# Three edits to a four-layer graph kernel: ScalarE issues the tile loads, the planner books the DMA engines, layer 3's product is split in three passes, and GpSimd alone adds the last h

## The chip, the cores and the metric

The kernel runs on one core of one Trainium2 chip. The metric is the device time of one execution in microseconds; the time of a kernel is the median of its runs. A profiled execution has a time of its own, a little beside that median.

## The reference

128 graphs of 128 nodes, 256 features each, float32, and a 0/1 adjacency matrix `adj` for each graph. Four layers follow each other, and each adds to x what it makes of h = relu(layernorm(x)):

- layer 0 is a gated graph network of three steps. In each step m = h W[i], the messages are summed over neighbours (`A^T m`), and a GRU cell with 768 gate columns makes the next h from the sums and from h. The last h is added to x.
- layer 1 is a relational sum: for every relation r of 4, a mask `adj == r` sums h over neighbours, and the sum goes through its own weight. With a 0/1 `adj` only r = 1 has any edges. A bias is added.
- layers 2 and 3 are graph attention: Wh = h W, scores e = leaky_relu(a1 Wh_i + a2 Wh_j), masked by `adj`, softmax over neighbours, and the weighted sum of Wh. They differ only in what a masked score becomes.

```python
x = x + _L0_gnn_ref(h, adj, weight, w_ih, w_hh, b_ih, b_hh)   # three GRU steps
x = x + _L1_gnn_ref(h, L1_adj, adj, L1_weight, L1_bias)       # masks (adj == r), r = 1..4
x = x + _L2_gnn_ref(h, adj, L2_W, L2_a)                       # attention, masked by -inf
x = x + _L3_gnn_ref(h, adj, L3_W, L3_a)                       # attention, masked by -9e15
```

## The kernel before

**Tiles.** Four graphs make a group (G = 4), so there are 32 groups, and a tile holds 128 partitions by 512 columns (T). In layer 0 the GRU's products are done with h turned, features on the partitions: `wide` tiles hold h so. In layers 1 to 3 a "duo" of two graphs shares one product (`product`, two graphs by 256 columns).

**Split products.** A float32 product on TensorE is emulated, where it matters, by three passes in the fp32r format: a matrix is split into a high part, a low part and their difference (`forms`: lines 944 to 966, `product`: lines 785 to 838). The high part is rounded by ScalarE or VectorE (L955, L957, L806, L808), the low part is made by VectorE (L961, L811) and the difference by GpSimd or VectorE (`difference`, L470). Passes 0 and 1 run, the result in PSUM is multiplied by 1 + 2^-12 (`rescale` L1011 and L1013 in layer 0, `scale` L828 and L830 in `product`, with a bias L1005), and pass 2 is added on top. All GRU gates are done so (L992, 216 passes of 512 columns a group). `THIN = (1, 2)` says that the products with the weights of layers 1 and 2 are done so too (L819, passes of 256 columns); layer 3's is a plain fp32 product (L775), whose left side is copied out of PSUM first (`evict`, L461). The last two groups (PLAIN) use plain products everywhere.

**Other steps that are named later.** L974 sums over neighbours in layer 0, L765 in layers 1 to 3. `norm` makes statistics on VectorE (L696 and the small steps L710 to L726), a power on GpSimd (L722) and the scaled relu on ScalarE (L743). The gates' tanh is on ScalarE (L1023, L1040), the GRU's update on VectorE (L1035, L1042, L1045, L1048). Attention scores are made on VectorE (L1119, L1170, L1173) and ScalarE (L1166, L1179), and VectorE adds the attention's result to x (L1210).

**Turns.** `turn` transposes 32x32 blocks on VectorE (L490), writes the tile to DRAM (`give`, L493) and reads it back with the blocks exchanged (`take`, L502, four DMAs). That is how h changes from features on partitions to nodes on partitions after each step, and how the attention matrix is turned. After the last step the turned h is added to x by VectorE or GpSimd, whichever the planner picks (`residual`, L1080).

**DMA queues.** Only SyncE issues DMAs, but for four weight loads at the start, which ScalarE issues. On SyncE's queue stand, in the planner's order: the loads of x (L513, twice for each group: once for layer 0 and, into another buffer, once again for the sum), of `adj` (L531, and again for the masks L524), of `adjT` (L1095), the turns, the row of attention terms that goes through DRAM (L1151, L1153), and the stores of the result (L1220). DMAs use eight completion semaphores in turn, so each waits until the one eight before it has landed. A load also waits until its buffer is free; there are three x buffers and five `adj` buffers, and an x buffer is often freed by the store of an earlier group.

**The order of the work.** No engine's order is written by hand. `build` records every operation with its engine (or a choice of engines), an estimate in ns and what it reads and writes. `Plan.order` then simulates the engines: it takes, again and again, the ready operation that could start first, and between operations of one engine that could start within `NEAR` ns the one with the lowest rank. The rank is made of the longest chain to the group's end, of the group's number times `PERIOD`, and of a table `OFFSETS` with a number for each place in the code, which was tuned. `LAG`, `HOP`, `OWN` and `late` say how long after an operation another engine, or the same one, sees its result; for a DMA, `LAG` says 4500 ns for SyncE and each call adds its own `late`. GpSimd's operations, and VectorE's operations with `port=True`, are planned so that they do not overlap (`port`). Up to `AHEAD` groups are in flight. The order that comes out is the order in which each engine's instructions are issued, and buffers are given out in it.

**Start and end.** While the weights are split, the whole of `adj` is scanned (L668, L670) for values over 1; a branch (L1236) then takes the program for 0/1 matrices, which is the one that runs, or a general one. The last group is worked in single graphs, the one before it in pairs, to shorten the end.

## Time and profile before

| | |
|---|---|
| median of 3 runs | 2342.71 us (2341.92 to 2347.65) |
| profiled execution | 2353.06 us, span 2351.2 us |
| TensorE matmul busy | 2291.9 us (97%), 12137 records |
| VectorE, ScalarE, GpSimd busy | 1978.2, 1582.0, 912.4 us |
| HBM | 114 GB/s over the span, DMA engines busy about half the time |

How to read it: an fp32 matmul leaves two records in the trace, a split pass one. Matmuls are pipelined, so their durations overlap and their sum is more than the time they take; the time from one start to the next is the pitch. "PEld" is the load of the stationary side, which overlaps the matmuls. Issues of DMAs are not counted as busy. A row of waits names who waited, at which line, for whom.

### The profile page before, as it was taken

The numbers are of one execution on the slowest core, as the hardware profiler recorded it, in microseconds if no ns is written. First come the engines' busy times: TensorE is split into PE (matmuls) and PEld (weight loads), VectorE is DVE, ScalarE is ACT, GpSimd is POOL, SyncE is SP. The second block draws the span as 40 slices with busy tenths as digits, with TensorE's granted clock in tenths as the row PEclk, the third lists the DMA queues.
The fourth block names the chain that finished last, engine by engine and source line by source line (L and its number), as shares of the span: only waits on it lengthen the run. The fifth ranks groups of instructions, "written<-read, shape, count | busy, mean of one in ns | idle before, by whom it ended". The sixth has DMA issues, their size and how long they took to land.

```text
span 2351.2 us, 39064 instructions
## 1 busy us (share of the span) xinstructions
PE 2291.9 (97%) x12137; PEld 1947.2 (83%) x12137; DVE 1978.2 (84%) x5405; ACT 1582.0 (67%) x3272; POOL 912.4 (39%) x729
## 2 busy tenths in 40 slices
PE   7999999999999999999999999999999999999997
PEld 6788888888888888888888888888888888788885
DVE  7858888888888888888888888888888888888887
ACT  6566676766676666666666766666766666666665
POOL 2334334443334443334343334343334343344421
PEclk9999999999999999999999999999999999999999
DMA  8535445555445455455455455455554555545431
GB/s 249 143 83 110 96 90 124 117 128 116 102 110 125 111 133 113 100 117 117 114 126 118 107 115 115 114 129 116 108 115 112 118 122 109 128 103 118 105 77 43
DMA packets 951273, 270.36 MB, mean 115 GB/s; under 512 B 677008, under 2 KB 939280, under 8 KB 951056
## 3 DMA queue, kind: packets, MB, share of 16 engines
q1 hardware_dynamic: 949968, 266.72, 50.0%
q8 instruction: 99, 1.62, 0.3%
q14 instruction: 118, 0.97, 0.2%
q10 hardware_dynamic: 1088, 1.05, 0.1%
HBM read 168.96 MB, written 98.69 MB: 114 GB/s over the span
## 4 chain that ended last, share of the span: by engine, by line
PE 64%; DVE 14%; DMA 10%; ACT 6%; SPq 4%; issue 3%; DVEq 0%; POOL 0%; ACTq 0%
PE bank L992 40%; PE bank L819 7%; PE bank L765 6%; PE bank L974 5%; PE bank L775 5%; DMA swap<-big 4%; SPq L502 4%; DMA big<-swap 3%; DVE junk L1119 3%; DVE form L961 2%; DMA wide<-swap 2%; ACT big L743 1%; DVE wide L1042 1%; DVE wide L1045 1%; DVE big L490 1%
## 5 line engine op out<-in xcount | busy, mean ns | idle before, releaser
L992 PE MATMUL bank<-form,wh_s 128*128 128x512 f32 x3456 | 953.4, 396 | 8.7 <-ACT bank L1005 4.6
L992 PE MATMUL bank<-form,wi_s 128*128 128x512 f32 x3456 | 944.0, 393 | 1.6 <-ACT bank L1013 0.9
L470 POOL TENSOR_TENSOR form<-form,form 128x512 fp32r<-128x512 f32 x383 | 517.7, 1362 | 800.4 <-DVE form L961 565.0
L992 PEld LDWEIGHTS bank<-form,wi_s 128*128 128x128 f32 x3456 | 644.1, 188 | 143.6 <-ACT bank L1013 3.1
L992 PEld LDWEIGHTS bank<-form,wh_s 128*128 128x128 f32 x3456 | 631.8, 188 | 151.5 <-ACT bank L1005 15.8
L1013 ACT ACTIVATE bank<-bank 128x512 f32<-128x512 f32 x448 | 255.4, 574 | 325.7 <-PE bank L992 324.4
L722 POOL TENSOR_TENSOR small<-small,nhalf 128x4 f32<-128x4 f32 (+2 forms) x140 | 142.2, 1020 | 408.8 <-DVE small L720 338.9
L1119 DVE CUSTOM_DVE_ANT_0 junk<-big,ub 128x256 bf16<-128x256 f32 x512 | 244.5, 478 | 14.2 <-ACT big L743 0.5
L743 ACT ACTIVATE big<-xs,small 128x256 f32<-128x256 f32 x384 | 200.1, 590 | 21.6 <-DVE small L726 12.2
L696 DVE BATCH_NORM_STATS2 small<-xs 128x6 f32<-128x256 f32 x512 | 190.0, 415 | 7.3 <-DMA xs<-in_x_dram 6.0
L470 POOL TENSOR_TENSOR cform<-cform,cform 128x512 fp32r<-128x512 f32 x120 | 155.2, 1294 | 96.2 <-DVE cform L811 83.0
L490 DVE STREAM_TRANSPOSE big<-wide 128x512 f32<-128x512 f32 x252 | 173.1, 697 | 4.0 <-ACT wide L743 2.3
L1035 DVE SCALAR_TENSOR_TENSOR bank<-big,bank 128x512 f32<-128x512 f32 x192 | 131.9, 690 | 48.5 <-PE bank L992 35.9
L955 ACT ACTIVATE form<-wide 128x512 fp32r<-128x512 f32 x179 | 109.2, 626 | 83.7 <-DMA wide<-swap 43.4
L1179 ACT ACTIVATE big<-big,small 128x128 f32<-128x128 f32 x256 | 99.8, 392 | 70.0 <-DVE small L1173 69.7
L1023 ACT ACTIVATE bank<-bank,b_rz 128x512 f32<-128x512 f32 x192 | 123.4, 655 | 34.0 <-PE bank L992 30.1
L1210 DVE SCALAR_TENSOR_TENSOR xs<-bank,small,xs 128x256 f32<-128x256 f32 x256 | 118.4, 475 | 31.6 <-PE bank L775 23.0
L1042 DVE TENSOR_TENSOR wide<-wide,bank 128x512 f32<-128x512 f32 x192 | 126.9, 682 | 21.4 <-ACT bank L1040 21.1
L765 PE MATMUL bank<-big,big 128*128 128x128 f32 x1024 | 130.7, 277 | 11.9 <-DVE wide L1045 7.1
L1023 ACT ACTIVATE big<-bank,b_rz 128x512 f32<-128x512 f32 x192 | 130.1, 681 | 16.3 <-PE bank L992 12.1
L765 PEld LDWEIGHTS bank<-big,big 128*128 128x128 f32 x1024 | 123.1, 192 | 19.4 <-DVE wide L1045 9.9
L974 PE MATMUL bank<-adjs,big 128*128 128x128 f32 x1024 | 131.2, 276 | 6.4 <-DMA big<-swap 5.1
(105 smaller groups left out, 3297.5 us busy)
## 6 DMA issues: line engine op xcount, KB each, us to landing
swap<-big SPq DMA_DIRECT2D x312, 256.0 KB, 2.5
big<-swap SPq DMA_DIRECT2D x992, 64.0 KB, 2.3
xs<-in_x_dram SPq DMA_DIRECT2D x128, 256.0 KB, 3.1
adjs<-in_adj_dram SPq DMA_DIRECT2D x64, 256.0 KB, 3.4
wide<-swap SPq DMA_DIRECT2D x128, 128.0 KB, 3.6
big<-line SPq DMA_DIRECT2D x60, 256.0 KB, 3.9
out_dram<-xs SPq DMA_DIRECT2D x30, 512.0 KB, 3.1
big<-in_adj_dram SPq DMA_DIRECT2D x32, 256.0 KB, 4.0
```

Source lines behind the costliest of these rows:

```text
L470: (nc.gpsimd if eng == "POOL" else nc.vector).tensor_tensor(at(df), at(lo).bitcast(F32), at(hi).bitcast(F32), ALU.subtract)
L490: nc.vector.transpose(part.t, src())
L696: op("DVE", dve(D), lambda g=g: nc.vector.bn_stats(s.t[:, ST + 6 * g : ST + 6 * g + 6], xt.t[:, g, :]), r=[(xt, {g})], w=[(s, {("mv", g)})])
L743: nc.scalar.activation(place(g), xt.t[:, g, :].rearrange("p (k m) -> p k m", k=KC), AF.Relu, bias=s.t[:, MR + g : MR + g + 1], scale=s.t[: ...
L765: nc.tensor.matmul(ps.t[:, (len(gs) * k + j) * P : (len(gs) * k + j + 1) * P], hs[g // 2].t[:, (g % 2) * D + k * P : (g % 2) * D + (k + 1) ...
L819: nc.tensor.matmul(po.t[:, j * D : (j + 1) * D], fs[f].t[:, (len(gs) * k + j) * P : (len(gs) * k + j + 1) * P], w.t[:, f, k, :], start=(st ...
L974: nc.tensor.matmul(pg.t[:, g * P : (g + 1) * P], of()[:, g * P : (g + 1) * P], flags(m0)[:, g * P : (g + 1) * P], start=True, stop=True,)
L992: nc.tensor.matmul(ps.t, w.t[(slice(None), *row, j, k, slice(c * P, (c + 1) * P))], b.t, start=(start and x == 0), stop=(x == len(terms) - ...
L1013: nc.scalar.mul(ps.t, ps.t, by)
L1023: op("ACT", act(T, 1), lambda: nc.scalar.activation(to.t, ps.t, AF.Tanh, bias=b_rz.t[:, c : c + 1], scale=0.5), r=[b_rz, *([ps] if kept el ...
L1042: op("DVE", dve(T), lambda c=c, ps=ps: nc.vector.tensor_tensor(hT.t[:, c, :], hT.t[:, c, :], ps.t, ALU.subtract), r=[ps], w=[(hT, {c})])
L1119: nc.vector.tensor_tensor_reduce(out=junk.t, in0=part, in1=ub[i].t[:, v, :], op0=ALU.mult, op1=ALU.add, scale=1.0, scalar=0.0, accum_out=s ...
```

## The change

- `QUEUE = "ACT"`: a new helper `arrive` issues the loads of x, `adj` and `adjT` (now at one line, `arrive`) from ScalarE's queue and not from SyncE's. The scan's loads, the other weights, the turns and the stores stay on SyncE.
- The planner keeps a time `engines` at which the DMA engines are free. An operation recorded for SP or ACTQ gets a size `dma` in ns (`moves`); it takes its place on them behind those placed before, and is seen `LAND` = 1400 ns, its own `late` and the usual hop later. An operation of another engine is seen at its end plus the usual hop; the loads are recorded for "ACT", with a `late` of `LANDING` = 4700 and `moves` = 800. The lags of 4500 and 2500 ns go. An issue is 530 ns and not 470, the estimates of ScalarE's and VectorE's operations rise by 6 or 7 ns, L1119's from 850 to 880, and a GpSimd operation may start `EASE` = 400 ns before VectorE's port is free in the plan.
- `THIN = (1, 2, 3)`: layer 3's product is split in three passes, and its weight with it.
- `residual` is GpSimd's alone.
- `PERIOD`, `CLOSE`, `SOON`, `NEAR` and all 24 rows of `OFFSETS` have new values, so the order of every engine is a new one.

```diff
 PE_COL = 430 / 512
-LAG = {"PE": 165, "ACT": 110, "DVE": 85, "POOL": 20, "SP": 4500, "ACTQ": 2500}
+LAG = {"PE": 165, "ACT": 110, "DVE": 85, "POOL": 20, "SP": 0, "ACTQ": 0}
 HOP = {"PE": 110, "ACT": 40, "DVE": 40, "POOL": 80, "SP": 100, "ACTQ": 100}
...
-OWN = {"PE": 0, "ACT": 125, "DVE": 125, "POOL": 80, "SP": 2500, "ACTQ": 2500}
-PERIOD = 29902
-CLOSE = 7183
+OWN = {"PE": 0, "ACT": 125, "DVE": 125, "POOL": 80, "SP": 0, "ACTQ": 0}
+PERIOD = 36412
+CLOSE = 18983
 CLOSING = 2
-SOON = -210
+SOON = 243
 AHEAD = 5
...
 SPLIT = 2
-LINE, SPREAD = 0, -1000
-GIVE = -400
-TAKE = -2500
+LAND = 1400
+LINE, SPREAD = 1300, 100
+GIVE = 0
+TAKE = 0
 TENSOR = ()
+ISSUE = 530
+EASE = 400
+LANDING = 4700
+ARRIVAL = 2300
+QUEUE = "ACT"
 BLOCK = 32
-NEAR = 69
+NEAR = 42
 RUSH = 90000
...
 DEEP = 1
-THIN = (1, 2)
+THIN = (1, 2, 3)
 LASTS = 4
...
 def seen(o, h):
-    return o.late + (LAG[o.eng] + HOP[h.eng] if h.engs != (o.eng,) else OWN[o.eng])
+    return (o.late + LAND + o.dma if o.dma is not None else 0) + (LAG[o.eng] + HOP[h.eng] if h.engs != (o.eng,) else OWN[o.eng])
...
 def act(n, ptrs=0):
-    return 50 + 95 * ptrs + 0.833 * n
+    return 57 + 95 * ptrs + 0.833 * n
...
 def dve(n):
-    return 68 + n / 0.96
+    return 74 + n / 0.96
...
 def dma(kb):
-    return 470
+    return ISSUE
...
 OFFSETS = {(stage, site): ns for stage, all_ in {
...
 }.items() for site, ns in enumerate(all_)}
...
 class Op:
-    __slots__ = ("engs", "eng", "times", "ns", "fn", "deps", "heirs", "bufs", "group", "key", "port", "rush", "late", "rank", "wait", "ready", "end", "most", "tag")
+    __slots__ = ("engs", "eng", "times", "ns", "fn", "deps", "heirs", "bufs", "group", "key", "port", "rush", "late", "dma", "rank", "wait", "ready", "end", "seen", "most", "tag")
...
-    def op(self, eng, ns, fn, r=(), w=(), after=(), port=None, rush=0, late=0):
+    def op(self, eng, ns, fn, r=(), w=(), after=(), port=None, rush=0, late=0, moves=None):
...
         o.rush, o.late, o.most = rush, late, self.most
+        o.dma = (300 if moves is None else moves) if o.engs[0] in ("SP", "ACTQ") else None
         if self.shared:
...
         at = dict.fromkeys(LAG, 0.0)
-        port = 0.0
+        port = engines = 0.0
...
         def place(o, eng, end):
-            nonlocal first, port
+            nonlocal first, port, engines
             for e in o.engs:
...
             o.end = at[eng] = end
+            o.seen = end
+            if o.dma is not None:
+                n = P // BLOCK if o.ns == ISSUE * P // BLOCK else 1
+                engines = max(max(engines, end - (n - 1) * ISSUE) + o.dma, end + o.dma / n)
+                o.seen = engines + LAND + o.late
             if o.port and eng != "ACT":
-                port = max(port, end)
+                port = max(port, end - (EASE if eng == "POOL" else 0))
             for b in o.bufs:
...
                 if not b.left and id(b.pool) in free:
-                    last = max(u.end + u.late + LAG[u.eng] + 60 for u, _, _ in b.uses)
+                    last = max(u.seen + LAG[u.eng] + 60 for u, _, _ in b.uses)
                     free[id(b.pool)][b.slot] = last
             for h in o.heirs:
-                h.ready = max(h.ready, o.end + seen(o, h))
+                way = LAG[o.eng] + HOP[h.eng] if h.engs != (o.eng,) else OWN[o.eng]
+                h.ready = max(h.ready, o.seen + way)
                 h.wait -= 1
...
                         continue
-                    start = max(at[eng], r, port if o.port and eng != "ACT" else 0)
+                    start = max(at[eng], r, port - (EASE if eng == "POOL" else 0) if o.port and eng != "ACT" else 0)
                     key = (start if start > at[eng] + NEAR else 0, o.rank)
...
                 op("DVE", dve(T) + 15, within, r=[r], w=[part])
-                op("SP", 470, give, r=[part], w=[(swap, {k})], late=GIVE)
+                op("SP", ISSUE, give, r=[part], w=[(swap, {k})], late=GIVE, moves=600)
...
-            op("SP", 470 * P // BLOCK, take, r=[swap], w=[w], late=TAKE)
+            op("SP", ISSUE * P // BLOCK, take, r=[swap], w=[w], late=TAKE, moves=1680 * n - 80 * (n - 1))
             return w
...
         state = {}
+
+        def arrive(dst, src, w, after=()):
+            on_act = QUEUE == "ACT"
+            op(QUEUE, dma(256), lambda: (nc.scalar if on_act else nc.sync).dma_start(out=dst(), in_=src), w=w,
+               after=after, late=LANDING if on_act else ARRIVAL, moves=800)
...
             for g2 in range(G // 2):
-                op("SP", dma(256), lambda g2=g2: nc.sync.dma_start(
-                    out=xt.t[:, 2 * g2 : 2 * g2 + 2, :],
-                    in_=x[ds(gi * G + 2 * g2, 2)].rearrange("g n d -> n g d")),
-                   w=[(xt, {2 * g2, 2 * g2 + 1})], after=after)
+                arrive(lambda g2=g2: xt.t[:, 2 * g2 : 2 * g2 + 2, :],
+                       x[ds(gi * G + 2 * g2, 2)].rearrange("g n d -> n g d"), [(xt, {2 * g2, 2 * g2 + 1})], after)
             return xt
...
             ai = Buf(adjs, f"again{gi}")
-            op("SP", dma(256), lambda: nc.sync.dma_start(
-                out=ai.t.rearrange("p (g j) -> p g j", g=G),
-                in_=adj[ds(gi * G, G)].rearrange("g i j -> i g j")), w=[ai], after=after)
+            arrive(lambda: ai.t.rearrange("p (g j) -> p g j", g=G),
+                   adj[ds(gi * G, G)].rearrange("g i j -> i g j"), [ai], after)
             return ai
...
             xt, ai = fetch(gi, "x0_"), Buf(adjs, f"adj{gi}")
-            op("SP", dma(256), lambda: nc.sync.dma_start(
-                out=ai.t.rearrange("p (g j) -> p g j", g=G),
-                in_=adj[ds(gi * G, G)].rearrange("g i j -> i g j")), w=[ai])
+            arrive(lambda: ai.t.rearrange("p (g j) -> p g j", g=G),
+                   adj[ds(gi * G, G)].rearrange("g i j -> i g j"), [ai])
             state[gi] = xt, ai
...
             if first:
-                op("ACTQ", dma(kb), lambda: nc.scalar.dma_start(out=dst(), in_=src), w=[buf])
+                op("ACTQ", dma(kb), lambda: nc.scalar.dma_start(out=dst(), in_=src), w=[buf], late=ARRIVAL, moves=3.1 * kb)
             else:
-                op("SP", dma(kb), lambda: nc.sync.dma_start(out=dst(), in_=src), w=[buf], rush=rush)
+                op("SP", dma(kb), lambda: nc.sync.dma_start(out=dst(), in_=src), w=[buf], rush=rush, late=ARRIVAL, moves=3.1 * kb)
...
             op("SP", dma(256), lambda part=part, f=f: nc.sync.dma_start(
-                out=part.t.bitcast(I32), in_=flat[:, f * T : (f + 1) * T]), w=[part])
+                out=part.t.bitcast(I32), in_=flat[:, f * T : (f + 1) * T]), w=[part], late=ARRIVAL, moves=800)
             op("DVE", dve(T), lambda part=part, f=f: nc.vector.tensor_reduce(
...
                 for k, h in enumerate(hs_new if i == L - 1 else ()):
-                    def residual(eng, k=k, h=h):
+                    def residual(k=k, h=h):
                         part = xt.t[:, :, k * P : (k + 1) * P]
-                        (nc.gpsimd if eng == "POOL" else nc.vector).tensor_tensor(
-                            part, part, h.t.rearrange("p (g d) -> p g d", g=G), ALU.add)
-
-                    op(("DVE", "POOL"), (dve(T), 1250), residual, r=[h], w=[(xt, set(range(G)))], port=True)
+                        nc.gpsimd.tensor_tensor(part, part, h.t.rearrange("p (g d) -> p g d", g=G), ALU.add)
+
+                    op("POOL", 1250, residual, r=[h], w=[(xt, set(range(G)))], port=True)
                 return [(h, lambda h=h: h.t) for h in hs_new]
...
             aiT = Buf(adjs, f"adjT{gi}")
-            op("SP", dma(256), lambda: nc.sync.dma_start(
-                out=aiT.t.rearrange("p (g j) -> p g j", g=G),
-                in_=adjT[ds(gi * G, G)].rearrange("g i j -> i g j")), w=[aiT], after=late)
+            arrive(lambda: aiT.t.rearrange("p (g j) -> p g j", g=G),
+                   adjT[ds(gi * G, G)].rearrange("g i j -> i g j"), [aiT], late)
...
-                    op("DVE", 850, terms, r=[(hs[g // 2], {g}), ub[i]], w=[junk, (s, {("ei", g)})], port=True)
+                    op("DVE", 880, terms, r=[(hs[g // 2], {g}), ub[i]], w=[junk, (s, {("ei", g)})], port=True)
                 for gs in pieces:
...
                     op("SP", 400, lambda: nc.sync.dma_start(out=line.t, in_=columns(EJ)),
-                       r=[terms], w=[line], late=LINE)
+                       r=[terms], w=[line], late=LINE, moves=0)
                     op("SP", 1280, lambda: nc.sync.dma_start(
                         out=pe.t, in_=line.t.rearrange("p g -> (p g)").partition_broadcast(P)),
-                       r=[line], w=[pe], late=SPREAD)
+                       r=[line], w=[pe], late=SPREAD, moves=1600)
...
                     out=out[ds(gi * G + gs.start, len(gs))].rearrange("g n d -> n g d"),
-                    in_=xt.t[:, gs.start : gs.stop, :]), r=[(xt, set(gs))])
+                    in_=xt.t[:, gs.start : gs.stop, :]), r=[(xt, set(gs))], moves=400 * len(gs))
```

## The prediction

> **What bounds the kernel now.** I read the page first (engine shares), then the stages by window, the waits of TensorE, its timeline inside one group, and last the groups and DMA rows that the moved work touches.
>
> ```profile
> PE 2291.9 (97%) x12137; PEld 1947.2 (83%) x12137; DVE 1978.2 (84%) x5405; ACT 1582.0 (67%) x3272; POOL 912.4 (39%) x729
> ```
>
> TensorE is busy 97% of a span of 2351.2 us; every other engine has at least 16% free.
>
> ```profile
> 0.00:20.00 20.00, 11.67 (x38) 9.44 (x39) 11.01 (x42) 9.17 (x25) 3.01 (x9) 0.93 1.00 292
> ...
> 20.00:40.00 20.00, 14.18 (x70) 11.99 (x70) 14.52 (x37) 17.46 (x52) 3.46 (x3) 0.93 0.82 220
> ...
> 500.00:1000.00 500.00, 493.71 (x2645) 421.91 (x2644) 428.10 (x1153) 338.40 (x693) 197.44 (x156) 1.00 0.52 116
> ...
> 2300.00:2352.00 52.00, 36.33 (x187) 28.73 (x185) 38.62 (x222) 27.61 (x84) 11.39 (x18) 0.90 0.17 48
> ```
>
> (stage, length, then busy of PE, PEld, DVE, ACT, POOL, the granted clock, DMA share, GB/s.) The middle loses 6 us of 500, the first 40 us lose 14 and the last 52 lose 16. But pipelined matmuls count as busy while the next waits, so I made a stricter ledger from the trace's matmul starts. Start to start, a split pass of 512 columns takes 0.2275 us, one of 256 columns 0.1165, an fp32 record of 256 columns 0.199 and of 128 columns 0.1115. 6912 x 0.2275 + 1440 x 0.1165 + 664 x 0.199 + 3169 x 0.1115 = 2226 us. The other 125 us are gaps: 28 before 110 us, 73 from there to 2214 us, 24 after it. The kernel is bound by matmul work, with 2.4 us of gaps in each of 30 groups (a period of 71 us).
>
> ```profile
> PEld bank L992 <- ACT bank L1005: 15.8, 26, 1.4
> ...
> PEld bank L992 <- DVE form L961: 10.1, 25, 0.9
> ...
> PE bank L765 <- DVE wide L1045: 7.1, 12, 1.5
> ...
> PE bank L974 <- DMA big<-swap: 5.1, 8, 1.5
> ```
>
> (who waited for whom: us, times, longest.) Counted by the gap ahead of each matmul that carries a wait: 11.4 us at L765 behind L1045 (23 of 32 cost 0.415 each), 9.4 behind the rescale L1005 (54 tight ones cost 0.158), 6.1 behind the low part L961 (4.3 of it where h is read from `wide`), 7.6 at L974 and L765 behind the turned tile's DMA. The other 38 us are spread in a few ns per matmul.
>
> **Layer 3's product.** In the built order 240 fp32 matmuls (480 records, 60 runs of 8) become 720 passes (60 runs of 12).
>
> ```profile
> 1064.21 1.89 PE L775 MATMUL bank<-wa,big 128*128 128x256 f32 x8
> 1065.75 1.28 PE L819 MATMUL bank<-w_s,cform 128*128 128x256 f32 x8
> ...
> 1070.94 1.09 PE L819 MATMUL bank<-w_s,cform 128*128 128x256 f32 x8
> 1071.87 1.08 PE L992 MATMUL bank<-form,wi_s 128*128 128x512 f32 x4
> ```
>
> A plain run takes 1065.75 - 1064.21 = 1.54 us, 8 passes 1071.87 - 1070.94 = 0.93, so 12 take 1.40. 60 x 0.14 = 8 us less on TensorE, on the path. Bounds: 0 with L819's mean pitch, waits included (0.130), and 12 with L775's mean (1.59 a run); I take the local reading. Beside TensorE it adds 60 low parts on DVE (0.68 us), 59 differences on POOL (1.29) and 60 rescales, nearly all ACT's (0.58). The third pass stands 0.9 us of matmul work or more behind the first two, as in layers 1 and 2, where such waits cost 0.032: +1 us.
>
> **The last h on GpSimd.**
>
> ```profile
> L1080 DVE TENSOR_TENSOR xs<-xs,big 128x512 f32<-128x512 f32 x47 | 40.9, 870 | 69.6 <-DMA big<-swap 66.5 <-issue 3.1
> ...
> L1080 POOL TENSOR_TENSOR xs<-xs,big 128x512 f32<-128x512 f32 x13 | 17.1, 1315 | 25.0 <-DMA big<-swap 21.1 <-ACT big L1179 2.8 <-DVE form L961 1.0
> ```
>
> 47 adds leave DVE, 41 us of work and 70 us in which it stood still for the turned tile. POOL gets 62 us and with the differences comes to about 1039 (44%). DVE stays near 1986, since 113 roundings of `wide` come to it from ACT (0.42 us each). Behind POOL's adds are queued its differences, with 7 us of cover. Nothing on the path.
>
> The row has these adds at 870 ns on DVE, against 672 for L1048, which has one input in PSUM. The Trainium skill, "SBUF — State Buffer", section "SBUF: two separate sides", speaks against the move: an instruction of VectorE or GpSimd with two SBUF inputs holds a shared port pair alone and blocks the other's for its whole length. This trace agrees (L1119 takes 422 ns clear of POOL's adds, 863 mostly beside them). Were all 62 us lost to TensorE, the sum would be 62 higher.
>
> **The loads on ScalarE.** 224 issues leave SyncE's queue for ACT's.
>
> ```profile
> 1.25 1.57 ACTq L542 DMA_DIRECT2D big<-in_wihT_dram  x3
> ...
> 2.84 1.28 ACT L580 ACT_TABLE_LOAD   x1 [2.84 <-issue]
> ```
>
> Three issues took 1.57 us of ACT, whose own first instruction started right after: 224 x 0.52 = 117 us. With +125 rescales, roundings and copies at 0.59 and -113 roundings at 0.626, ACT comes to 1700 us, 72%. The issue itself costs TensorE little. What costs is where the readers stand. The new planner books transfer time only for operations named SP or ACTQ; the loads are named ACT, so `o.dma` is None, `late` is not used, and the plan has the tile there 0.15 us after the issue. The trace has
>
> ```profile
> xs<-in_x_dram SPq DMA_DIRECT2D x128, 256.0 KB, 3.1
> adjs<-in_adj_dram SPq DMA_DIRECT2D x64, 256.0 KB, 3.4
> ```
>
> 3.1 to 3.6 us. In the built order of before, the first reader stands far behind: as matmul work between what the load and what the reader's predecessor on its engine depend on, 11.3 us for the statistics L696 and 14 for L849 (medians). Now it is 0.9 and 0: ACT issues the `again` load and its very next instruction is L849, which reads it; L854 follows its load by 1.8; DVE reaches L696 just after the issue. Before, L696 hardly ever waits:
>
> ```profile
> L696 DVE BATCH_NORM_STATS2 small<-xs 128x6 f32<-128x256 f32 x512 | 190.0, 415 | 7.3 <-DMA xs<-in_x_dram 6.0 <-POOL xs L1080 0.3
> ```
>
> Worked out for one group of the new order, with durations of this trace: L849 holds ACT for 3.6 us; the rescale L830 behind it has its matmuls 6.3 us later, so it ends just in time (0 to 0.8 us lost). L854 holds ACT 2 us, before a tanh with 2.3 us of cover (0 to 0.5). DVE is worse. Its two L1210, a low part and two statistics end 2.7 us after TensorE's release; the x load is issued by ACT 0.8 us after it, behind an adj load and a rounding, and lands 3.1 later: DVE stands 1.2 us. Behind it are queued four statistics, the mask, L1035, two L1210 and L811, on which TensorE's next product waits with 2.05 us of cover and 0.9 to spare: about 1 us lost, and 0.15 more at the L828 after it. That x load also waits for the store of an earlier tile, which costs SyncE now
>
> ```profile
> SPq L513 <- DMA out_dram<-xs: 69.9, 25, 4.4
> ```
>
> 2.8 us a time. If DVE is 1 us late, all of this comes 1 us later. I take 1.3 us lost in each of 28 groups, +36. Bounds: -5 (DVE's and ACT's free time takes it all, and SyncE's turns are no longer queued behind the loads' waits) and +84 (3 us, a whole landing, each time).
>
> **The rest of the new order.** Everything moves, so I counted in both built orders the matmul work between what a waited-for instruction depends on and the matmul that waits; this is cover, not time. L765 behind L1045 goes from 3.6 us to 5.4, where two waits of before cost nothing: -11 (to 0). h from `wide` is rounded by DVE without a hop: -4 (to 0). L765's turned tile goes from 9.6 to 10.9 us of cover, L974's from 9.6-11.4 to 9.5-15.9: -4 (-8 to +8). L1005's tight waits stay, 54 before and 50 after. New is L1035 with 2.7 us 29 times; three such cost 0.218 each: +3 (0 to +9).
>
> Start: ACT's first computing instructions are twelve L743 for three groups, the last of which need the 24th transfer; in the start's timeline the 24th is issued at 14.9 us and lands near 20. The splits of the weights (L580), which begin at 8.4 us now, are queued behind them and begin near 24; ACT's 30 us of splits before the first rescale end near 54, and not 46. Later stalls of the start get fewer: +7 (-2 to +14). Close: 38 us of matmul work after the last gate pass against 39: 0 (-6 to +6).
>
> **Sum.** -8 +1 +36 -11 -4 -4 +3 +7 = +20. The profiled execution took 2353.06 us (span 2351.2), 10.4 above the median of the runs, 2342.71; the difference goes over: 2363 us.
>
> **Rivals.** (1) Faster: the landings are hidden. DVE has 16% and ACT 28% free; if what is queued behind a late load has more cover than I counted, the sum without that term is -16: 2327. It decides at 16/28 = 0.6 us a group. For it: the plan's waits carry their cover on top of a chain that the trace shows shorter. Against: the 0.9 us to spare above. (2) Much slower: DVE runs late as now, where the store is issued 3.6 to 5 us after its last matmul and not 1.2; then a whole landing is lost in each group: -16 + 84, 2411. (3) No change: about 0.6 us a group, 2343. That the change does not do what it says is excluded by the order: no tile load is left on SyncE, no L1080 on DVE, no `wa` in L775.
>
> **How the numbers follow.** Forecast 0.48 (2350 to 2380), hidden 0.22, no change 0.13, much slower 0.17. 0.3% is 7 us, about what a measurement of this kernel can tell from no change. Faster by more 0.22; within it 0.13; slower by more 0.65. The range reaches into the first and second rival: 2324 to 2396.
>
> **What would show it.** Right: L696 waits for in_x_dram in nearly every group, 1 to 2 us each; ACT at L849 and L854 waits for in_adj and in_adjT, some 5 us a group; L819 on `wa` in runs of 12 at 1.40 us; no wait L765 behind L1045; new gaps at L819 behind L811. Wrong: those waits there and the middle's gaps under 60 us (rival 1), or gaps of over 4.5 us a group (rival 2).

## The result, and the profile after

The kernel after took 2397.28 us (median of four runs, 2395.05 to 2400.24) against 2343.34 beside it: a ratio of 1.0226, 95% interval 1.021 to 1.0242, or 54 us more. The forecast was +20 to 2363, with a range to 2396. The profiled execution took 2398.08 us (span 2396.2), so the two profiles differ by 45 us; the other 9 come from the profiled run of before, which stood 10.4 us over its own median. Gaps read from that profile are therefore somewhat larger than those of a usual run.

The page's shares, as read before:

```profile
PE 2296.9 (96%) x12377; PEld 1946.7 (81%) x12377; DVE 2044.1 (85%) x5478; ACT 1596.9 (67%) x3291; POOL 1047.9 (44%) x827
```

GpSimd was put near 1039 us, and came to 1048. DVE was put near 1986, and came to 2044: nobody gave it 58 us of work, so something makes its instructions longer. That is the thread to pull; the group shown below accounts for 57 of the 58.

The same windows (start, length, then busy PE, PEld, DVE, ACT, POOL, the granted clock, the DMA share, GB/s):

```profile
0.00:20.00 20.00, 0.46 (x2) 0.47 (x2) 5.97 (x27) 2.40 (x4) 2.38 (x9) 1.00 0.96 282
20.00:40.00 20.00, 18.29 (x77) 15.12 (x76) 16.36 (x46) 17.25 (x52) 4.00 (x4) 1.00 0.26 79
500.00:1000.00 500.00, 493.86 (x2720) 421.26 (x2719) 444.39 (x1171) 343.54 (x698) 239.84 (x185) 1.00 0.51 116
```

TensorE does next to nothing in the first 20 us. In the middle its busy share hardly differs from before, which is why the prediction did not trust that column. The stricter ledger (start of each matmul less the matmul work in front of it) says more:

| us of gaps | before | after | difference |
|---|---|---|---|
| up to 100 us of matmul work | 28.0 | 42.0 | +14 |
| from there to 1955 us of work (27 groups) | 65.3 | 88.2 | +23 |
| from there to the last matmul | 26.1 | 46.1 | +20 |
| matmul work | 2225.8 | 2214.2 | -11.6 |

The waits of the whole span answer to those shown of before (who waited for whom: us, times, longest):

```profile
ACT adjs L867 <- DMA adjs<-in_adj_dram: 43.8, 30, 6.6
ACT adjs L872 <- DMA adjs<-in_adjT_dram: 33.1, 30, 2.9
...
DVE small L714 <- DMA xs<-in_x_dram: 30.8, 34, 4.9
...
PEld bank L1010 <- DVE bank L1029: 19.6, 22, 1.3
...
PEld bank L837 <- DVE cform L829: 18.9, 22, 2.8
```

The first three are the landings that the prediction announced (L849, L854 and L696 of before). The fifth is its new gap behind the low part. The fourth, TensorE behind a rescale on DVE, was not in it at all. And the group on DVE that grew:

```profile
L1189 DVE CUSTOM_DVE_ANT_0 big<-big,adjs 128x128 f32<-128x128 f32 x256 | 120.8, 514 | 1.0
```

This is the masked minimum of the attention, with two inputs in SBUF (L1173 of before). In the profile of before the same 256 instructions read

```profile
L1173 DVE CUSTOM_DVE_ANT_0 big<-big,adjs 128x128 f32<-128x128 f32 x256 | 63.3, 299 | 1.0
```

### The profile page after: what moved, and what is told of

The parts are those of the page before. It is cut to its first block, busy times and chain, and to the rows that moved or that the text cites. A ratio compares the mean times of both kernels' runs of the same rounds, so it can differ in the third digit from the quotient of the medians.

```text
span 2396.2 us, 39659 instructions
## 1 busy us (share of the span) xinstructions
PE 2296.9 (96%) x12377; PEld 1946.7 (81%) x12377; DVE 2044.1 (85%) x5478; ACT 1596.9 (67%) x3291; POOL 1047.9 (44%) x827
## 5 line engine op out<-in xcount | busy, mean ns | idle before, releaser
L487 POOL TENSOR_TENSOR form<-form,form 128x512 fp32r<-128x512 f32 x375 | 506.6, 1361 | 711.3 <-DVE form L979 622.4
L1031 ACT ACTIVATE bank<-bank 128x512 f32<-128x512 f32 x471 | 270.9, 579 | 285.6 <-PE bank L1010 282.6
L487 POOL TENSOR_TENSOR cform<-cform,cform 128x512 fp32r<-128x512 f32 x179 | 236.4, 1321 | 226.9 <-DVE cform L829 184.4
L740 POOL TENSOR_TENSOR small<-small,nhalf 128x4 f32<-128x4 f32 (+2 forms) x140 | 136.0, 972 | 336.5 <-DVE small L738 309.5
L1135 DVE CUSTOM_DVE_ANT_0 junk<-big,ub 128x256 bf16<-128x256 f32 x512 | 222.3, 434 | 34.7 <-ACT big L761 11.0
L837 PE MATMUL bank<-wa,cform 128*128 128x256 f32 x1440 | 228.4, 293 | 16.1 <-DVE cform L829 8.3
L837 PEld LDWEIGHTS bank<-wa,cform 128*128 128x128 f32 x1440 | 196.3, 191 | 45.1 <-issue 17.1
L714 DVE BATCH_NORM_STATS2 small<-xs 128x6 f32<-128x256 f32 x512 | 188.3, 412 | 33.8 <-DMA xs<-in_x_dram 30.8
L979 DVE SCALAR_TENSOR_TENSOR form<-form,bank 128x512 fp32r<-128x512 f32 x192 | 130.3, 680 | 63.7 <-ACT form L973 62.5
L848 ACT ACTIVATE bank<-bank 128x512 f32<-128x512 f32 x154 | 89.4, 581 | 117.3 <-PE bank L837 110.8
L973 ACT ACTIVATE form<-bank 128x512 fp32r<-128x512 f32 x184 | 106.7, 597 | 69.6 <-PE bank L992 69.2
L979 DVE SCALAR_TENSOR_TENSOR form<-form,wide 128x512 fp32r<-128x512 f32 x192 | 146.2, 772 | 0.0
```

The source lines that it names most:

```text
L487: (nc.gpsimd if eng == "POOL" else nc.vector).tensor_tensor(at(df), at(lo).bitcast(F32), at(hi).bitcast(F32), ALU.subtract)
L714: op("DVE", dve(D), lambda g=g: nc.vector.bn_stats(s.t[:, ST + 6 * g : ST + 6 * g + 6], xt.t[:, g, :]), r=[(xt, {g})], w=[(s, {("mv", g)})])
L740: op("POOL", 1000, lambda: nc.gpsimd.tensor_tensor(columns(RS), columns(RS), nhalf.t[:, gs.start : gs.stop], ALU.pow), r=[nhalf], w=[own(" ...
L837: nc.tensor.matmul(po.t[:, j * D : (j + 1) * D], fs[f].t[:, (len(gs) * k + j) * P : (len(gs) * k + j + 1) * P], w.t[:, f, k, :], start=(st ...
L979: op("DVE", dve(T), lambda: nc.vector.scalar_tensor_tensor(lo.t, f(hi), -1 / UNIT, src(), ALU.mult, ALU.add), r=[dep, hi, token], w=[lo], ...
L1031: nc.scalar.mul(ps.t, ps.t, by)
```

## The experiments

Each starts from the built order of one of the two kernels and changes one thing in it, or two, since any new run of the planner moves everything. Where instructions are moved, this function sorts the list by planned start plus a delay, and keeps every dependence and every reuse of a tile:

```python
def later(issue, cut, by):
    key, seen, slots = {}, {}, {}
    for n, o in enumerate(issue):
        k = max([o.end - o.times[o.engs.index(o.eng)] + (by(o) if n >= cut else 0)] + [key[id(d)] for d in o.deps])
...
    return issue[:cut] + sorted(issue[cut:], key=lambda o: key[id(o)])
```

The runs stood on several chips, and on two of them the kernel before itself took 2363 to 2365 us and not 2344. So kernels are compared by their ratio to the kernel before on the same chip; 0.001 is 2.3 us.

| kernel | ratio to before, 95% interval |
|---|---|
| after | 1.0226 (1.021 to 1.0242); on a slower chip 1.0193 (1.0166 to 1.0221) |
| ScalarE's readers later | 1.0187 (1.0169 to 1.0206) |
| first norm later | 1.072 (1.0699 to 1.0741) |
| both later | 1.0679 (1.0659 to 1.0699) |
| loads issued by SyncE | 1.0303 (1.0282 to 1.0324) |
| statistics on another tile | 1.0155 (1.0127 to 1.0182) |
| no landing waited for | 1.0071 (1.005 to 1.0092) |
| layer 3 loosened | 1.0159 (1.0137 to 1.018) |
| no landing, layer 3 loosened | 0.9999 (0.9983 to 1.0016) |
| start in another order | 1.0208 (1.0188 to 1.0229) |
| no last add | 1.0026 (1.0014 to 1.0038) |
| GpSimd copies | 1.0064 (1.0041 to 1.0087) |
| GpSimd fills | 1.0039 (1.0024 to 1.0053) |
| last add on DVE | 1.0085 (1.0059 to 1.0111) |
| last add on DVE, ScalarE's readers later | 1.0036 (1.0024 to 1.0047) |
| before, adds on GpSimd | 1.0066 (1.0047 to 1.0085) |
| before, loads issued by ScalarE | 1.0079 (1.006 to 1.0097) |
| before, all adds on DVE | 1.0004 (0.9989 to 1.0019) |

### The landings

ScalarE's readers, moved back by 8 us:

```diff
     issue, cut = plan.order(pools, big, verdict)
+    def by(o):
+        if o.tag[0] % 10 == 4 and o.eng == "ACT" and o.ns != ISSUE and o.bufs[0].name[:4] in ("agai", "adjT"):
+            return 8000
+        return 0
+    issue = later(issue, cut, by)
```

> The kernel after, with one thing moved: in each group the two ScalarE instructions that read a tile just issued (L867 on the second copy of adj, L872 on adjT) stand 8 us of plan time later in ScalarE's order; nothing else changes place. Their results are first read 59 and 62 us of plan time later, so nothing gets late by it. In the profile after, ScalarE stands 43.8 + 33.1 us at these two lines; that must go. Theory (readers that stand right behind their loads): the prediction gave these two waits 0 to 1.3 us of each of 28 groups and took a small part of it, so -5 us (-36 to 0). Rival 1 (the new gaps come from the third passes of layer 3 and from rescales given to DVE, whatever the loads do): within 2 us of after, and the gaps at L837 in layer 1 stay near 20 us. Rival 2 (the issuing itself on ScalarE costs): within 2 us as well.

It took 2387.19 us, 10 less than after. The rows L867 and L872 are gone from its waits. By the ledger the middle gave back 4.5 us and the last groups and the close 8.

The statistics that open a group, reading a tile that is there:

```diff
-                    s.t[:, ST + 6 * g : ST + 6 * g + 6], xt.t[:, g, :]),
+                    s.t[:, ST + 6 * g : ST + 6 * g + 6], b1s.t if h0 and int(nm[2:]) > 4 else xt.t[:, g, :]),
```

> The kernel after with one operand changed: from the sixth group on, the four statistics L714 that open a group read the bias tile, which has been on the chip since the start, and not the tile of x just loaded (so the outputs of these groups are not the reference's). Nothing changes place and the instruction's size is the same. DVE's wait for x at L714 (30.8 us in the whole span, 19.6 of it between 150 and 2060 us) goes. The prediction put about 1.15 us of each of 28 groups on this wait, -32 us. From the later run in which ScalarE's two readers stood further back (2387.2, -10 us), the gaps behind L829 (L837, 16 us in the middle) were not touched and should shrink now. Theory: -20 us (-32 to -8). Rival 1 (the order as such: rescales on DVE, third passes): -3 to +3. Rival 2 (issue on ScalarE): -3 to +3.

2379.31 us, 18 less. In its profile the middle's gaps went from 88.2 to 73.6 us, and those of the last groups fell by 7. Both edits together:

> The kernel after with both: ScalarE's readers L867 and L872 stand 8 us of plan time further back, and the opening statistics L714 read the bias tile from the sixth group on (so those groups' outputs are not the reference's). No engine waits for a landing in the middle any more. Theory (two separate engines, each held up on its own): the two single runs add, -10 - 18 = -28 us, 2369 (2361 to 2377). Rival (both hold up the same chain, so that the second finds it freed already): about -18, 2379.

The ratio was 1.0071, 0.0122 to 0.0155 under after by which of after's two ratios is taken: 29 to 36 us. The two add up, with nothing shared. So the landings cost 28 to 36 us of the 54.

The other way to take DVE's wait away was to move the norm, not its data:

```diff
+        if o.tag[0] % 10 == 0 and o.ns != ISSUE:
+            return 2500
```

> The kernel after, with the whole first norm of each next group (mask L950, statistics L714, moments, power, relu L761 and the turns of its h) 2.5 us of plan time later in the order, so that the statistics stand 3.3 us and more behind the load of x and not 0.8 to 1.3. In the profile after, DVE stands 30.8 us at L714 and 15.2 at L950. Theory: the prediction put 1.15 us of each of 28 groups on this wait, so -32 us if it was right; from the ledger of after, whose middle has about 39 us of new gaps and 20 of them at L837 in layer 1, -15 is more likely (-32 to -5). Rival 1 (third passes and rescales): within 3 us of after. Rival 2 (issue on ScalarE): within 3 us.

It missed by far: 2511.53 us, 114 more. With ScalarE's readers moved as well it was no better:

> Both moves together. Theory: all landing waits of DVE and ScalarE in the middle are gone, 2397 - 36 = 2361 by the prediction's term, about 2377 by the gaps seen at L837 in layer 1 (20 us against 1.8 before). Rival 1: 2397 within 4 us, since the chain of rescale, low part and difference in the three layers sets the gaps. Rival 2: 2397 within 4 us.

2504.1 us. The waits of the first of the two show why:

```profile
PE bank L837 <- DVE small L738: 41.7, 22, 1.9
```

Moved by 2.5 us, the norm's statistics and small instructions came to stand in front of a rescale (L846) that the planner had given to DVE; TensorE's third passes behind that rescale lost about 2 us in each of 22 places, 45 us and not 5. That is a third of the 111 us of gaps that the middle gained; 18 more stand behind the rescale L1029, and the rest is spread. A late reader is not mended by moving it without looking at what it then stands in front of.

### Who issues

After's list, with SyncE as the issuer:

```diff
-            op(QUEUE, dma(256), lambda: (nc.scalar if on_act else nc.sync).dma_start(out=dst(), in_=src), w=w,
+            op(QUEUE, dma(256), lambda: nc.sync.dma_start(out=dst(), in_=src), w=w,
```

> The kernel after, its list of operations unchanged, with the 224 loads of x, adj and adjT issued by SyncE at the same places of the list. ScalarE loses 224 issues (59.8 MB on its queue, some 0.4 to 0.5 us each) and its waits for free tiles; the readers still stand right behind the loads. Theory: the landing waits stay, and time stays within 10 us of 2397 (later if loads queue behind turns on SyncE). Rival 2 (the issue on ScalarE is what costs): 15 to 40 us less, and the start 10 us earlier, since ScalarE's first L761 no longer stands behind 12 issues until 16 us. Rival 1: within 5 us.

2413.81 us, 16.5 more, though the start got 6 us shorter (gaps of 36.2 and not 42.0 at 100 us of matmul work). ScalarE's wait at L867 between 150 and 2060 us went from 33.1 to 92.0: queued behind SyncE's turns the loads come later still, though a load of `adj` takes no longer from issue to landing there (2.9 us against 3.0). What ScalarE does next is then late too: TensorE's gaps behind its rescale L848 grew from 5.9 to 27.1 us in the middle. Before's list, with ScalarE as the issuer from the sixth group on:

```diff
-                op("SP", dma(256), lambda g2=g2: nc.sync.dma_start(
+                op("SP", dma(256), lambda g2=g2: (nc.scalar if gi > 4 else nc.sync).dma_start(
```

> The kernel before, its list of operations unchanged, with the loads of x, adj and adjT from the sixth group on issued by ScalarE at the same places of the list; the readers keep their 11 and 14 us of cover. The prediction (issuing on ScalarE costs TensorE little): 0 to +8 us. Rival 2 (issue on ScalarE, 0.5 us each and waits for free tiles in its order): +20 to +45, as much as the whole change.

2360.11 us, 16 more: twice the upper end of what the prediction's reading allowed, and short of the 20 that the rival asked for. It does not show as TensorE waiting for ScalarE: the middle's gaps behind the rescale L1005 fell from 8.8 to 3.8 us. TensorE waits more often for turned tiles:

```profile
PE bank L974 <- DMA big<-swap: 14.0, 16, 2.2
```

In the profile of before this row has 5.1 us, 8 times. Loads and turned tiles used to follow one another in SyncE's queue; now they can be under way side by side. The Trainium skill, "DMA: Bandwidth & Descriptors", section "Queues, rings and completion order", says that the two queues are rings on the same 16 DMA engines, not engines of their own. So the loads might slow the turns, but the times from issue to landing hardly show it: between 100 and 2200 us a turned tile's write takes 2.60 us (median) and was 2.53, its read 2.27 and was 2.31. Why the tiles come late for TensorE these runs leave open. Under a fixed order the change of issuer costs 16 us in either direction; the order is built for one of them.

### The last add on GpSimd

Before's list with its 47 adds on DVE issued on GpSimd:

```diff
-                        (nc.gpsimd if eng == "POOL" else nc.vector).tensor_tensor(
+                        nc.gpsimd.tensor_tensor(
```

> The kernel before, its list of operations unchanged, with the 47 last adds of h to x that its planner gave to DVE issued on GpSimd at the same places. The prediction: nothing on the path, 0 us (-5 to +5), though DVE loses 41 us of work and 70 of standing. Rival (port shared by two engines, all 62 us of POOL's adds lost): up to +60.

2357.66 us, 14 more. Its rows:

```profile
L1173 DVE CUSTOM_DVE_ANT_0 big<-big,adjs 128x128 f32<-128x128 f32 x256 | 109.2, 477 | 1.0
...
DVE small L696 <- POOL xs L1080: 78.7, 25, 5.1
...
PEld bank L765 <- DVE wide L1045: 27.1, 22, 2.5
```

In the profile of before the last of these rows is

```profile
PEld bank L765 <- DVE wide L1045: 9.9, 14, 1.7
```

The masked minimum went from 299 to 477 ns, and L765's wait for L1045, the very gap that the change removes, grew. But in this run VectorE's statistics also stand 78.7 us for the adds themselves, against 0.3 before, so it does not tell a slowed instruction from a late one. In after, the readers of x wait for the add 2 times, 2.5 us in all.

In after, with the add left out from the sixth group on:

```diff
+                        if gi > 4:
+                            return
                         nc.gpsimd.tensor_tensor(part, part, h.t.rearrange("p (g d) -> p g d", g=G), ALU.add)
```

> The kernel after with the last add of h to x (L1096) left out from the sixth group on, its transfers kept (so the outputs lack h). POOL loses 54 of its 60 adds of 1.3 us and the port pair it shares with DVE is free in that time. The prediction (nothing on the path): 0 to -3 us. Rival (the port: DVE's instructions with two inputs in SBUF stand beside the adds): -10 to -30 us.

The ratio fell to 1.0026, 39 to 47 us less than after, more than the rival's 10 to 30. Three runs then took the add apart on one chip, where after had 1.0193:

```diff
-                        nc.gpsimd.tensor_tensor(part, part, h.t.rearrange("p (g d) -> p g d", g=G), ALU.add)
+                        nc.gpsimd.tensor_copy(part, h.t.rearrange("p (g d) -> p g d", g=G))   # GpSimd copies
+                        nc.gpsimd.memset(part, 0.5)                                          # GpSimd fills
+                        nc.vector.tensor_tensor(part, part, h.t.rearrange("p (g d) -> p g d", g=G), ALU.add)   # on DVE
```

(each from the sixth group on, in a kernel of its own).

> The kernel after, unchanged, as the reference for the three runs beside it: ratio to the kernel before 1.0226 as on the first chip (1.021 to 1.0245).

2408.08 us, a ratio of 1.0193, under the 1.021 to 1.0245 expected though the intervals meet; L1189 at 514 ns again.

> The kernel after with the last add of h (L1098) replaced, from the sixth group on, by a GpSimd copy of h over x (so these groups' outputs lack x): the same tiles written, the same waits, one input in SBUF and not two. The masked minimum L1189 on DVE took 299 ns before, 514 after and 348 without the add. Theory A (port, taken by any GpSimd instruction that reads SBUF): L1189 stays over 420 ns on average and the time within 12 us of after_here. Theory B (the wait of x's readers for the add, or GpSimd's queue): within 12 us of after_here as well, but with L1189 near 350. Theory C (port, taken by two inputs alone): L1189 near 350 and 20 to 45 us less.

> The same with a GpSimd fill in place of the copy (outputs of these groups lack x and h): the tile is written at the same place of GpSimd's order, its readers still wait for it, and nothing is read from SBUF. Theory A: L1189 near 350 ns or less, L1010's waits for the rescale L1029 (10.5 + 19.6 us in after) nearly gone, 20 to 45 us less than after_here. Theory B, as far as it is the order and x's readers: within 12 us of after_here.

> The kernel after with the last add of h issued on DVE from the sixth group on, at the same place of the list. DVE gets 54 adds of 0.87 us, 47 us of work, in front of the statistics that read x, and loses the stretching of L1189 (256 x 0.17 to 0.2 us, some 45 us). Theory A: about even on DVE, so -10 us (-25 to +5). Theory B: DVE's order is dense, and 0.87 us more in it twice a group costs +15 to +40.

They took 2378.49, 2371.78 and 2381.59 us: 30, 36 and 26 less. The masked minimum (group on DVE, ns each after the second comma) with the copy, the fill and the add on DVE:

```profile
L1192 DVE CUSTOM_DVE_ANT_0 big<-big,adjs 128x128 f32<-128x128 f32 x256 | 89.2, 390 | 1.0
```

```profile
L1192 DVE CUSTOM_DVE_ANT_0 big<-big,adjs 128x128 f32<-128x128 f32 x256 | 77.4, 346 | 1.0
```

```profile
L1192 DVE CUSTOM_DVE_ANT_0 big<-big,adjs 128x128 f32<-128x128 f32 x256 | 77.0, 343 | 0.2
```

The fill keeps the write to x and its readers' wait, reads nothing, and brings back about what leaving the add out does. That speaks against theory B, not conclusively, since the fill is also shorter (530 ns against 1498) and does not wait for h. Two rows of after itself say more: the 2.5 us above, and 0.1 us of TensorE's gaps in the middle that end with one of GpSimd's differences. The copy was expected to go with A or with C, and lies between: one input still stretches L1189 (390 against 346 ns), by about a quarter of what the add does, in about half of the add's time (812 ns). What shows the mechanism is the 256 minima of after, sorted by what GpSimd did meanwhile: 174 beside nothing took 281 ns on average, 54 beside an add 1159, 27 beside a difference (L487) 737. In the two other kernels they took 538 beside a copy (47 of them) and 290 beside a fill (44). The wait is for GpSimd's reading, then, and not for its order. One such place in the timeline of after (start, us, engine, line):

```profile
1056.20 2.91 PE L1010 MATMUL bank<-form,wi_s 128*128 128x512 f32 x12
...
1056.45 3.05 POOL L1098 TENSOR_TENSOR xs<-xs,big 128x512 f32<-128x512 f32 x2
...
1057.08 1.27 DVE L1189 CUSTOM_DVE_ANT_0 big<-big,adjs 128x128 f32<-128x128 f32 x1
...
1058.28 1.37 DVE L1189 CUSTOM_DVE_ANT_0 big<-big,adjs 128x128 f32<-128x128 f32 x1
...
1059.58 0.28 DVE L1189 CUSTOM_DVE_ANT_0 big<-big,adjs 128x128 f32<-128x128 f32 x1
...
1059.79 0.69 DVE L1029 TENSOR_SCALAR bank<-bank 128x512 f32<-128x512 f32 x1
...
1060.53 1.31 PE L1010 MATMUL bank<-form,wi_s 128*128 128x512 f32 x4 [0.50 <-DVE bank L1029]
```

Two adds hold GpSimd from 1056.45 to 1059.50. Two minima on DVE end 0.16 and 0.15 us behind the first and the second, after 1.27 and 1.37 us; the third, alone, takes 0.28. The rescale L1029 queued behind them comes 0.99 + 1.09 = 2.1 us later than it could, more than its cover of 1.8 us, and TensorE stands 0.50 us for it. This is no single case: the middle has 20 gaps behind L1029, 13.8 us in all, and in front of 18 of them stand two such minima. With the copy and the fill the gaps there sum to 0.8 and 1.5 us, with the add on DVE to 5.2.

That is a part of the cost. From the unchanged after on that chip to the fill, the middle's gaps go from 97.7 to 63.9 us: 11.2 of the 33.8 stood behind L1029, 9.2 behind turned tiles at L992, 4.6 behind the low part L829, and the rest in smaller pieces. With the add on DVE they go to 72.7.

Before's 13 adds on GpSimd, on the other hand, given to DVE by the inverse edit:

> The kernel before, its list unchanged, with the 13 last adds of h that its planner gave to GpSimd issued on DVE at the same places. If an add on GpSimd costs what the kernel after shows (about 27 us for 50 adds, 0.53 each), 13 of them give back up to 7 us: ratio 0.997 (0.995 to 1.001). Rival (the planner put these 13 where VectorE was needed by others): +2 to +8 us, 1.001 to 1.0035.

Ratio 1.0004, interval 0.9989 to 1.0019: no gain that can be seen. In the trace of before only 4 of the 256 minima and 2 of the 512 instructions L1119 stand beside one of those 13 adds; the planner had put them where they cost next to nothing, and the expectation had priced all adds alike.

### Layer 3's third passes

```diff
-                difference(fs[2], fs[1], fs[0], lambda b: b.t[:, :N], N, [place])
+                difference(fs[2], fs[1], fs[0], lambda b: b.t[:, :N], N, [place], layer == 3)
...
-                                    fs[f].t[:, (len(gs) * k + j) * P : (len(gs) * k + j + 1) * P],
+                                    fs[1 if layer == 3 and f == 2 else f].t[:, (len(gs) * k + j) * P : (len(gs) * k + j + 1) * P],
...
                 def scale(eng):
+                    if layer == 3:
+                        return
```

(`difference` returns at once where its last argument is true.)

> The kernel after with layer 3's product loosened: its difference and its rescale are left out, and the last four of its 12 passes read the low part again and not the difference (so the output lacks a correction). TensorE does the same 12 passes in the same places; POOL loses 59 differences of 1.3 us, ScalarE nearly all of 60 rescales of 0.6 us, and the third passes wait for nothing new. Theory (landings): the third passes cost about what the prediction said, +1 us, so -2 us (-8 to 0; the gaps at L837 in layer 3 are 7.5 us in the middle). Rival 1 (the chain of low part, difference and rescale in three layers is what costs): -15 to -30. Rival 2: -5 to -10 by 35 us less work on ScalarE.

2382.78 us, 14.5 less, against 2 expected. And on top of the landings:

> The same with layer 3's difference and rescale left out too (its last four passes read the low part again). Theory: landings and the third passes' chain are separate costs, so 2369 - 14 = 2355 (2348 to 2362). Rival (the third passes' chain only came late because DVE and ScalarE had been held up by landings): the single run's -14 shrinks to -3 or less here, 2366 or more.

Ratio 0.9999, 17 us under the run without it. It doesn't shrink when the landings are gone, so it is a cost of its own. L1189 still takes 516 ns in the first of them, so it doesn't go by way of the masked minimum. Whether it is the wait of the third passes, ScalarE's 35 us of rescales or GpSimd's 77 us of differences, these runs don't tell apart.

### The start

```diff
+        if n(o) < cut and o.tag[0] == 0 and o.group in (1, 2, 3) and o.end < 24000:
+            return 14000
+        if n(o) < cut and o.eng == "PE" and o.tag[0] == 21 and o.end < 10000:
+            return 8000
```

(with `later` sorting the part ahead of the verdict too).

> The kernel after with the start in another order: loads and first norms of groups 1 to 3 stand 14 us of plan time later, and the first group's gathers stand behind six products of the weights, as they do in the kernel before; from the verdict on, the order is that of after. Theory (ScalarE issues loads until 16 us and then works at L761 for three groups, so the splits of the weights and TensorE begin late): TensorE's first matmul near 6 us and not 19.3; of the 14 us that the start lost against before, 8 to 12 come back, 2387 (2383 to 2392). Rival (the start is bound by the transfers of the weights and by splits, whatever the order): within 3 us of 2397.

The ratio is 1.0208 on a slower chip, inside the interval that after had on another slower one (1.0166 to 1.0221) and just under the first (1.021 to 1.0242). TensorE's first matmul did come at 8.75 us and not 19.54, but at 100 us of matmul work its gaps were 48.2 us and not 42.0. The rival held: this other order does not mend the start. Of its 14 us, 6 go with the issues on ScalarE (the run with SyncE); the other 8 stay open.

### The two costs together

The last add on DVE and ScalarE's readers moved back, in one kernel that leaves nothing out:

> The kernel after with two things changed at once: the last add of h on DVE from the sixth group on (alone: ratio to before from 1.0193 to 1.0085 on one chip, -26.5 us), and ScalarE's readers L867 and L872 8 us of plan time later (alone: 1.0226 to 1.0187, -10 us). Theory (separate costs): ratio 1.0045, 1.002 to 1.008, so nearly all of the change's loss comes back with the third passes and the start as they are. Rival (both relieve the same wait): 1.008 to 1.011.

Ratio 1.0036, interval 1.0024 to 1.0047: the costs add, and two small edits give back 0.0157 to 0.019, 37 to 45 us. Its window in the middle (columns as above):

```profile
500.00:1000.00 500.00, 496.78 (x2743) 425.08 (x2743) 440.24 (x1187) 344.03 (x700) 220.23 (x173) 1.00 0.51 117
```

TensorE is busy 496.78 us of 500, against 493.86 in after. By the ledger the middle's gaps are 65.4 us. Its chip was one of the slower ones; there the kernel before with all its adds on DVE, as fast as before itself, had 77.3, and the unchanged after had 97.7 on another slower chip. No kernel that leaves nothing out came under the kernel before.

## Why the prediction was right in sign and short by 34 us

- **The last h on GpSimd: put at nothing, cost 26 us** against the same add on DVE, and 36 against none that reads. This is the step that failed. The prediction asked who waits for GpSimd and found 7 us of cover. It named the Trainium skill, "SBUF — State Buffer", section "SBUF: two separate sides", which says that a VectorE instruction with two SBUF inputs and a GpSimd instruction that reads SBUF exclude each other for a whole instruction, and said that 62 us would be lost if all of it came to TensorE. But it gave this no term, no rival and no chance, and no reason for leaving it out: it did not ask which VectorE instructions stand beside the adds and what is queued behind them. Both prices, 0 and 62, were wrong; the rule was not: 0.28 us became 1.27 and 1.37, and DVE's free 16% did not help, because a rescale with 1.8 us of cover stood in line behind. Its reading of the trace was loose as well: of the 65 instructions behind its 863 ns, 53 stood beside GpSimd's differences and 2 beside an add of h.
- **The third passes: put at +1, cost some 15** together with their differences and rescales. The price was taken over from layers 1 and 2, 0.032 us a wait; which of the three costs it stays open. With 8 to 12 us less matmul work, layer 3's part as a whole brings nothing; the prediction had -7.
- **The landings: put at +36, measured 28 to 36.** The planner's blindness to loads named ACT, the readers behind them and the rows that would show it were all as said. The split was not quite: DVE's statistics 18 us, 0.64 a group and not 1.15; ScalarE's two readers 10, mostly in the last groups, where no term stood. That the total came out is in part luck.
- **Layer 3's product: -8.** By the pitches of the ledger -11.6, the upper bound given. The passes stand as 8 and 4, apart, and not in runs of 12.
- **Waits removed: -11 at L765 behind L1045** (L783 and L1063 now): 9.5 us gone, as said. L961: all its 6.1 in the middle gone, against 4. L1005, which was to stay, lost its 9.4 us as well; in its place came L1029 with 13.8, by the port. L1035's tight waits cost nothing, against 3.
- **The start: +7, was +14**, the end of its bounds. **The close: 0**; the ledger has +20 from the 28th group on, 8 of it ScalarE's landings. The rest of it stays open.
- **Issuing on ScalarE** costs little as work: 0.38 to 0.44 us an issue by the trace's records, some 94 us where 117 were reckoned. **The turned tiles**, put at -4 by their cover, brought nothing: the middle's gaps behind them were 7.7 us and are 8.3.

With the measured values the sum is -12 + 15 + 26 + 28 - 10 - 6 - 9 + 14 = +46, against +45 between the two profiles and +54 between the medians. It is an account, not a proof: it mixes times of runs with gaps of single profiles, of which that of before is 10 us long, the single effects were measured in orders in which the others were present, and the last groups' remainder stands in none of them.

Of what would show it: L714 waits in 34 places, 0.9 us each, against 1 to 2; ScalarE stands 2.6 us a group and not 5; no wait is left at L783 behind L1063; the new gaps behind L829 are there (14.4 us in the middle). The middle's gaps were 88.2 / 27 = 3.3 us a group, between the forecast and the second rival's 4.5.

## What to carry to other kernels

When work moves to GpSimd, list VectorE's instructions with two inputs in SBUF that run beside it, and what is queued behind them with little cover; GpSimd's own queue says nothing on that. When a DMA changes its issuer, look at where its first reader stands and at what is queued behind that reader. In an order that is tuned as a whole, test a part by changing one operand or one engine in place; a shift of 2.5 us that looked harmless cost 114 us.

## What the runs showed that was not expected

- A masked minimum of 0.28 us (two SBUF inputs) took 1159 ns on average beside GpSimd's adds, 538 beside a GpSimd copy with a single input, and 290 beside a fill, which reads nothing.
- An issue on ScalarE takes 0.4 us in the middle. In the first 20 us, where the DMA share is 0.96, two issues took 3.93 us, others stood apart by 1 us and more, and ScalarE's first computing instruction came at 16 us, after 14 issues:

```profile
9.73 3.93 ACTq L529 DMA_DIRECT2D adjs<-in_adj_dram  x2
...
15.98 1.28 ACT L761 ACT_TABLE_LOAD   x1 [15.98 <-DMA small<-in_a_dram]
```

- Chips differ: the same kernel before took 2344 us on some and 2363 to 2365 on others, while the ratio of after to before moved only from 1.0226 to 1.0193.
